# A fused cross-attention kernel on one core: the same operations by another table of turns

## The chip, the core and the metric

The kernel runs on one core of a Trainium2 chip. A core has five engines with a queue of instructions each: TensorE (PE in the profile; its weight loads are listed apart as PEld), VectorE (DVE), ScalarE (ACT), GpSimd (POOL) and SyncE (SP, which only issues transfers here). Each engine works through its queue in order and waits on semaphores where it needs another's result. Matrix products are written to PSUM, in banks of 128 x 512 float32. The metric is the time of one launch in microseconds of the device; less is better.

## The reference

Two batches of 2048 rows of 640 (`x`), and 128 rows of context of 384 per batch, the last four of which are "adapter" tokens. There are 8 heads of 80. All of it is float32. Cut to what matters:

```python
query = x @ Wq;  keyt = enc[:, :124] @ Wk;  valt = enc[:, :124] @ Wv
hs = mha(query, keyt, valt)                        # text: 2048 x 124 scores per head
ca = enc[:, 124:]
ca_q1 = einsum('btc,th->bch', ca, Wq_ca)[:, indices]   # 2048 rows, picked from 384
ca_hs1 = mha(ca_q1, x, x)                          # adapter: against the 2048 rows of x
ca_hs2 = mha(ca_hs1 @ Wq, ca @ Wk_ca, ca @ Wv_ca)  # 4 tokens
out = (hs + ca_hs2) @ Wout + b_out + x
```

Only 384 rows of the adapter's queries differ, so the kernel computes these and adds the right one to each row of the output at the end, by an indirect transfer of GpSimd.

## The kernel before, in words

**Work.** After a setup (weights turned and rearranged, text keys and values, 0 to about 60 us) the rows of `x` come in eight blocks of 512. Each block gives the adapter's two operands (`pyz`, `yz`, `zop`, `y_sb`) and the queries (`pq`, summed by reads into the tile `q`). The text attention works in 16 units of 256 rows, each with two halves of 128 ("softmax" tasks): scores `sc` on PE, row maxima `m` on DVE, exponentials with their sums on ACT (`p`), reciprocals `r` on DVE, then the shares (`p` times `r`; the function `share` may run on POOL, DVE or ACT), a transposition on DVE (`eb`), a store and a turned reload (`kept`, `pT`) through DRAM on SP. Then PE multiplies the probabilities by the values (`ph`), and ACT or DVE copies these into `hs`.

**Output.** For each unit the products of `hs` with `Wout` (`po`) and, for most blocks, those of the queries (`pq`) are made with seven half-size products instead of eight. That needs sums of quarters beforehand (`hs` sums s1 to s4, `wout_sums`, `x_sums`, each by POOL or DVE) and additions of results into the rows afterwards (DVE, `last_rows` and `x_more`). The rows begin as the residual, loaded by SP; when a tile of 128 rows has all its additions, POOL adds the adapter's rows by an indirect transfer (`add_second`, DMA_INDIRECT in the profile), and SP or ACT issues the store to the output.

**Adapter.** For each batch (`adapter`) PE makes scores twice. The first time, four 512-wide products (`s`) into one four-bank tile that exists once (`quad`), of which DVE takes the maxima (`mx`) and frees the tile; 24 of these groups for each batch. The second time ACT exponentiates the tile (`ea`), and PE contracts it with `y_sb` (`acc`); again 24 groups.

**Shapes of the PE array.** PE is used as tiles of 128x32, 32x128, 64x128, 64x32 or 128x128 rows and columns; `pq`, `po`, `ph` and `acc` are 128x32, the adapter's `s` is 32x128, the text scores `sc` 64x128, transpositions 128x128.

**What sets the order.** The tasks are Python generators that yield operations (`Do`) to a planner, `Desk`, which emits the instructions. Every operation belongs to a task with a path (`.56.3` is the third fork of the 56th task), and the table `TURNS` has for each path a list of turns, one for each operation of the task. A turn is one number that says two things: turn modulo 6 is the engine (PE, ACT, DVE, POOL, SP, or NONE for an operation without an instruction), and the order of turns is the order of emission, hence of each engine's queue. `run` takes the waiting operation with the lowest turn and gives it to `issue`, which emits it and keeps a planned time. That planned time decides one thing on the chip: `Room.take` gives an operation those buffers (PSUM banks, row slots, tiles) that the planner thinks are free earliest. All waiting on the chip is by semaphores that follow the data.

The paths that the prediction's steps touch:

- `.55.1`: the first scores and maxima of the adapter of the second batch (from about 280 us); turns 8022, 8160 and 8298 are the score groups at 305.82, 309.49 and 313.15 us.
- `.54`: the fifth column product of the last block's queries; `.54.7.3`: one of its chains; `.56.3`, `.60.3`, `.58.3`: the `ph` products of units 0, 4 and 2; `.68.2` and `.67.2`: text scores.
- `.60.3.4`: the sum s3 of `hs` of unit 4; `.60.3.12` and `.60.3.13`: the `po` products at 334.24 and 332.30 us.
- `.76.1` to `.76.4`: the four `wout_sums`.
- The last step of `stored` (paths such as `.62.3.10`): the stores of the output, "ACT" or "SP".

Every vector, scalar and GpSimd instruction shows line 427 in the profile (the helper `__getattr__`), products show 396 (`matmul`) or 405 (`by_columns`), transpositions 410, transfers 447 (`dma`), and GpSimd's indirect transfer 2351. So tiles are told apart by their names.

Of the kernel before, what the change touches and what calls it, by code (L numbers as in the profile page):

```python
# [8 lines left out]
F32 = mybir.dt.float32  # L9
# [5 lines left out]
P = 128  # L15
# [44 lines left out]
class Task:  # L60
    def __init__(self, gen, rank, key, more):
        self.gen, self.rank, self.key, self.more, self.last = gen, rank, key, more, Event()
        self.forks, self.ops, self.path = 0, 0, ""


class Desk:
# [242 lines left out]
    def begin(self, gen, rank):  # L309
        name = gen.__name__  # L310
        n = self.begun[name] = self.begun.get(name, -1) + 1
# [77 lines left out]
    def streamed(self, rhs):  # L389
        n = 1  # L390
# [69 lines left out]
def kernel(  # L460
# [15 lines left out]
    B, S, H = x.shape  # L476
# [2115 lines left out]
```

## Time and profile before

| | before |
|---|---|
| median of three runs | 573.39 us (572.63 to 573.96) |
| span of the profiled execution | 571.3 us |
| the profiled execution's own whole time | not given; the median is 2.1 us above the span |
| PE busy | 563.6 us (99%), 8069 instructions |
| DVE, ACT, POOL busy | 394.4, 286.7, 159.8 us |
| maxima of the adapter (`mx`) | 48 of 2271 ns on DVE |
| exponentials of the adapter (`ea`) | 48 of 1884 ns on ACT |
| DMA | 113.21 MB, 198 GB/s on average |

The profile gives one execution. Busy time is the union of an engine's instructions; ends of matrix products are modelled, so small stalls of PE do not always show as idle time. In a row of the timeline stand the start, the length, the engine, the line of the kernel, the operation, output and inputs, the shape, and the number of instructions put together; a bracket says how long the engine idled before it and who released it. In a table by stage each engine has its busy time within the stretch.

### The profile page before, as it was taken

To read this page: it belongs to the slowest core of one execution; us is meant where nothing else is said; L and a number is where in the kernel's file an instruction comes from. 1 tells how busy PE (TensorE), PEld (TensorE's weight loads), DVE (VectorE), ACT (ScalarE), POOL (GpSimd) and SP (SyncE) were. 2 spreads that over 40 slices of the span, in tenths; PEclk is the share of its full clock that TensorE was granted. 3 is DMA by queue.
4 is the path that set the end of the run, shared out by engine and by line. 5 is a ranking of instruction groups with operands and counts; after the bars stand their busy time and mean duration, and the time that the engine had idled before them with its cause. 6 is when DMAs were issued, how large, how long until landed. Compare 5 with 4: busy or idle time off the path is not lost.

```text
span 571.3 us, 18875 instructions
## 1 busy us (share of the span) xinstructions
PE 563.6 (99%) x8069; PEld 310.0 (54%) x8069; DVE 394.4 (69%) x659; ACT 286.7 (50%) x806; POOL 159.8 (28%) x213
## 2 busy tenths in 40 slices
PE   9999999999999999999999999999999999999997
PEld 8885335455555455466554554554555554445553
DVE  4366999999998577458999999998332213544443
ACT  2021355645566899899876654524554664100000
POOL 9102041114440731100004350531203053045152
PEclk9999999999999999999999999999999999999999
DMA  8998576965968977446746969977476587799888
GB/s 246 211 248 126 139 161 157 172 179 139 211 212 153 215 182 211 146 126 198 233 158 203 316 180 319 245 217 230 96 263 120 164 206 223 248 211 213 258 156 237
DMA packets 145691, 113.21 MB, mean 198 GB/s; under 512 B 82548, under 2 KB 116980, under 8 KB 145608
## 3 DMA queue, kind: packets, MB, share of 16 engines
q1 hardware_dynamic: 137000, 95.10, 60.0%
q0 software_dynamic: 5632, 10.69, 11.7%
q10 hardware_dynamic: 2976, 6.23, 3.2%
q8 instruction: 63, 1.03, 0.8%
q14 instruction: 20, 0.16, 0.1%
HBM read 71.60 MB, written 40.39 MB: 196 GB/s over the span
## 4 chain that ended last, share of the span: by engine, by line
PE 92%; DVE 3%; ACT 3%; DMA 1%; issue 1%; SPq 0%; ACTq 0%; DVEq 0%
PE po L405 27%; PE pq L405 24%; PE sc L396 7%; PE acc L396 7%; PE s L396 7%; PE ph L396 6%; PE pq L396 4%; PE pyz L396 2%; ACT ea L427 2%; DVE mx L427 2%; PE pv L396 1%; PE pk L396 1%; DMA xz<-in_x_dram 1%; ACT p L427 1%; PE pt_wq L410 1%
## 5 line engine op out<-in xcount | busy, mean ns | idle before, releaser
L427 ACT ACTIVATE p<-sc,m 128x124 f32<-128x124 f32 x256 | 90.1, 381 | 43.4 <-DVE m L427 38.4
L427 DVE TENSOR_REDUCE mx<-s 128x4 f32<-128x2048 f32 x48 | 109.0, 2271 | 1.9 <-PE s L396 1.9
L427 ACT ACTIVATE ea<-s 128x2048 f32<-128x2048 f32 x48 | 90.5, 1884 | 31.4 <-PE s L396 30.9
L405 PE MATMUL po<-wout_sums,hs 128*32 128x320 f32 x1024 | 78.5, 434 | 0.1
L405 PE MATMUL po<-wout_sb,hs 128*32 128x320 f32 x928 | 72.4, 433 | 0.0
L427 POOL TENSOR_TENSOR p<-p,r 128x992 f32<-128x992 f32 x17 | 31.4, 1847 | 130.9 <-DVE r L427 130.9
L405 PE MATMUL pq<-xt,wq_sb 128*32 128x256 f32 (+1 forms) x928 | 66.4, 418 | 0.0
L427 DVE TENSOR_TENSOR last_rows<-last_rows,po 128x320 f32<-128x320 f32 x60 | 28.1, 480 | 44.0 <-PE po L405 43.9
L427 ACT ACTIVATION_READ_ACCUMULATOR p<-sc,m 128x1 f32 x256 | 57.0, 223 | 0.0
L427 DVE TENSOR_TENSOR x_more<-x_more,po 128x320 f32<-128x320 f32 x68 | 32.4, 481 | 34.5 <-PE po L405 32.5
L405 PEld LDWEIGHTS po<-wout_sums,hs 128*32 128x32 f32 x1024 | 33.4, 110 | 32.7 <-issue 2.8
L427 DVE TENSOR_REDUCE m<-sc 128x4 f32<-128x496 f32 x64 | 40.8, 663 | 14.1 <-PE sc L396 14.0
L396 PE MATMUL acc<-ea,y_sb 128*32 128x384 f32 (+2 forms) x768 | 50.2, 382 | 0.2 <-ACT ea L427 0.2
L396 PE MATMUL ph<-pT,vpad 128*32 128x256 f32 x768 | 47.9, 381 | 0.0
L405 PEld LDWEIGHTS po<-wout_sb,hs 128*32 128x32 f32 x928 | 30.1, 110 | 28.2 <-issue 1.6
L2351 POOL DMA_INDIRECT x_more<-o,query x17 | 26.6, 1563 | 67.0 <-DVE x_more L427 31.1
L405 PEld LDWEIGHTS pq<-xt,wq_sb 128*32 128x32 f32 x928 | 27.7, 110 | 28.0 <-issue 13.4
L427 ACT COPY hs<-ph 128x512 f32<-128x512 f32 (+1 forms) x25 | 13.4, 551 | 57.7 <-PE ph L396 57.7
L427 DVE STREAM_TRANSPOSE eb<-p 128x1024 f32<-128x1024 f32 x32 | 39.4, 1233 | 1.2 <-POOL p L427 1.1
L396 PEld LDWEIGHTS sc<-kmain,q 64*128 64x128 f32 x512 | 31.8, 187 | 12.6 <-issue 5.8
L427 POOL TENSOR_TENSOR hs<-hs 128x256 f32<-128x256 f32 x31 | 28.9, 1019 | 33.9 <-ACT hs L427 25.6
L396 PE MATMUL sc<-kmain,q 64*128 64x124 f32 x512 | 38.0, 285 | 0.0
(219 smaller groups left out, 835.0 us busy)
## 6 DMA issues: line engine op xcount, KB each, us to landing
kept<-eb SPq DMA_DIRECT2D x32, 512.0 KB
pT<-kept SPq DMA_DIRECT2D x16, 1024.0 KB
landing<-away SPq DMA_DIRECT2D x15, 512.0 KB
xi<-in_x_dram SPq DMA_DIRECT2D x56, 128.0 KB
x_more<-in_x_dram SPq DMA_DIRECT2D x17, 320.0 KB
last_rows<-in_x_dram SPq DMA_DIRECT2D x15, 320.0 KB
y<-yt SPq DMA_DIRECT2D x16, 256.0 KB
y_sb<-y SPq DMA_DIRECT2D x32, 128.0 KB
```

Source lines behind the costliest of these rows:

```text
L396: self.pin(self.nc.tensor.matmul(out, lhsT, rhs, **kw))
L405: self.pin(self.nc.tensor.matmul(out[j : j + 32], lhsT[:, j : j + 32], rhs, **kw))
L410: self.pin(self.nc.tensor.transpose(out, in_, ident))
L427: self.pin(getattr(engine, what)(*args, **kw))
L2351: desk.pin(nc.gpsimd.indirect_dma_start(out=t, out_offset=None, in_=o2_of[b], in_offset=bass.IndirectOffsetOnAxis(ap=query[:, st : st + 1] ...
```

## The change

The table `TURNS` is replaced from turn 1141 on. The turns before are the same. 2281 turns stand in 617 paths, and 2021 of them have another number. 89 operations change their engine:

| from | to | number | what |
|---|---|---|---|
| ACT | DVE | 20 | copies of `ph` into `hs`, first reads of `pq`, two spreads of the text values, two copies of the adapter's result |
| DVE | POOL | 19 | sums of `hs`, of `x` and of `Wout`, two shares |
| POOL | DVE | 17 | the same kinds, two shares among them |
| DVE | ACT | 15 | copies and reads, one share |
| ACT | SP | 12 | stores of the output |
| ACT | POOL | 4 | shares |
| POOL | ACT | 1 | a share |
| SP | ACT | 1 | a half store of the output |

All others keep their engine, and many change their place in its queue. The planner is changed too: an operation without instruction holds back the later ones of its task and its forks (`placed`), planned times no longer rise with the turn (`run`), and some costs are other numbers (`streamed`; issue costs and latencies of transfers, of which a few are shown). The instructions emitted for an operation are the same.

```diff
-        self.forks, self.ops, self.path = 0, 0, ""
+        self.forks, self.ops, self.path, self.placed = 0, 0, "", None
...
+        task.placed = self.parent.placed
...
+        if task.placed is not None:
+            op.wait.append(task.placed)
+        if op.engines == ("NONE",):
+            task.placed = op.at
...
-            self.issue(max(self.ready(op), self.free[engine], self.now), engine, op)
+            self.issue(max(self.ready(op), self.free[engine]), engine, op)
...
-        return (max(n / 1.2, 106 if self.mode[1] > 32 else 27) + (9 if self.mode == (64, P) else 2.5)) / 1e3
+        return (max(n / 1.193, 106 if self.mode[1] > 32 else 27) + (9 if self.mode == (64, P) else 2.5)) / 1e3
...
-                    by_tokens[a], 0.67, 0.38, 1.7,
+                    by_tokens[a], 0.67, 0.56, 2.0,
...
-                dma(t, x[b, st * P : (st + 1) * P, :], 1.06, 0.37, 1.85)
+                dma(t, x[b, st * P : (st + 1) * P, :], 1.06, 0.38, 1.55)
...
-        desk.transfer("POOL", 2.0, 1.57, 2.2)
+        desk.transfer("POOL", 2.0, 1.57, 1.7)
```

The entries of the table that the text speaks of, each written on a line of its own (in `.55.1` the turns of the score groups and maxima around 300 to 318 us only):

```diff
-  ".54": [6215, 7055, 7373, 7812, 7968, 8040, 8057]
+  ".54": [5933, 7223, 7835, 7836, 7866, 7986, 8447]
-  ".54.7.3": [7740, 7902, 7932]
+  ".54.7.3": [7740, 7902, 8058]
-  ".55.1": [... 8022, 8048, 8160, 8222, 8298, 8324 ... 9234, 9284, 9318 ...]
+  ".55.1": [... 7980, 7994, 8166, 8174, 8262, 8270 ... 9264, 9272, 9354 ...]
-  ".56.3": [3275, 7079, 7132, 8100, 8124, 8184, 8339]
+  ".56.3": [7109, 7115, 7462, 8154, 8196, 8202, 8243]
-  ".60.3.4": [8870]        # DVE
+  ".60.3.4": [8745]        # POOL
-  ".60.3.12": [8898, 9086, 9108, 9152]
+  ".60.3.12": [8850, 8900, 8976, 8996]
-  ".60.3.13": [8844, 8906]
+  ".60.3.13": [8826, 8834]
-  ".67.2": [7650, 7854]
+  ".67.2": [7626, 7800]
-  ".67.3": [8543, 12509, 12520, 12966, 12978, 12990, 13001]
+  ".67.3": [9455, 12791, 12808, 12888, 12900, 12918, 12965]
-  ".76.1": [8150], ".76.2": [8115], ".76.3": [8205], ".76.4": [8277]
+  ".76.1": [8091], ".76.2": [8151], ".76.3": [8097], ".76.4": [8216]
-  ".62.3.10": [11069, 11085, 11161]   # a store, ACT
+  ".62.3.10": [11171, 11373, 11380]   # SP
```

More of the change, by code (lines that the diff above doesn't have):

```diff
@@ L1143, in keys @@
                     lambda i=i, e=e: dma(
-                        away[:, i, e].rearrange("q (g n) -> q g n", g=4), z[:, e].bitcast(F32), 0.45, 0.45
+                        away[:, i, e].rearrange("q (g n) -> q g n", g=4), z[:, e].bitcast(F32), 0.45, 0.6
                     ),
@@ L1272, in values_weights @@
             yield Do(
-                "SP", lambda g=g, cols=cols: dma(w2_sb[G * g : G * (g + 1)], rows_w2[:, :, cols], 0.45, 0.42),
+                "SP", lambda g=g, cols=cols: dma(w2_sb[G * g : G * (g + 1)], rows_w2[:, :, cols], 0.45, 0.62),
                 [("w2 out", g) for g in range(4)], marks=[("w2", g)],
@@ L1361, in of_pairs @@
                 d1 = VR + (R * i + VH) % P
-                dma(most[part, :2], v[:, 0::2, :, d0 : d0 + R], 1.7, 1.31)
+                dma(most[part, :2], v[:, 0::2, :, d0 : d0 + R], 1.7, 1.5, 1.6)
                 desk.pin(nc.sync.dma_start(most[part, 2:], v[:, 1::2, :, d1 : d1 + R]))
@@ L1369, in between_pairs @@
                     g = (0, 2, 1, 3)[i]
-                    dma(rest[part], w[:, :, D2 * g - VR : D2 * g + VR], 0.42, 0.45)
+                    dma(rest[part], w[:, :, D2 * g - VR : D2 * g + VR], 0.42, 0.95, 1.5)
                 else:
-                    dma(rest[part, :, :VR], w[:, :, H - VR :], 0.28, 0.46)
-                    dma(rest[part, :, VR:], w[:, :, :VR], 0.28, 0.46)
+                    dma(rest[part, :, :VR], w[:, :, H - VR :], 0.28, 0.8, 1.6)
+                    dma(rest[part, :, VR:], w[:, :, :VR], 0.28, 0.8, 1.6)
             op = yield Do("SP", between_pairs, [])
@@ L1709, in part_away @@
             def part_away(i, k=k, z=z):
-                dma(away[k, :, i].rearrange("q (g n) -> q g n", g=4), z[:, i].bitcast(F32), 0.48, 0.45, 1.6)
+                dma(away[k, :, i].rearrange("q (g n) -> q g n", g=4), z[:, i].bitcast(F32), 0.48, 0.59, 1.75)
             op = yield Do("ACT", lambda: desk.a_copy(z[:, 0], pq[:, cols]), [at], rank=0)
@@ L1736, in rest_back @@
         yield Do(
-            "SP", lambda: dma(t.rearrange("p g n -> p (g n)"), by_rows, 2.0, 0.56), [op.at], marks=[("landed", m)],
+            "SP", lambda: dma(t.rearrange("p g n -> p (g n)"), by_rows, 2.0, 0.6, 1.7), [op.at], marks=[("landed", m)],
             rank=0,
@@ L1848, in away @@
             def away(t=op.value, u=u):
-                dma(kept[:, :, u, :], t.rearrange("p (a n) -> p a n", a=4), 0.9, 0.53, 1.6)
+                dma(kept[:, :, u, :], t.rearrange("p (a n) -> p a n", a=4), 0.9, 0.58, 1.65)
             yield Do("SP", away, frees=[(yts, op.slots[0][0])], marks=[("y out", b, sb, u)], rank=0.5)
```

394 rows, old and new, of the table TURNS are left out of this document.

## The prediction

> **What bounds the kernel now.** I read the page's head, its tenths and its chain first.
>
> ```profile
> span 571.3 us, 18875 instructions
> PE 563.6 (99%) x8069; PEld 310.0 (54%) x8069; DVE 394.4 (69%) x659; ACT 286.7 (50%) x806; POOL 159.8 (28%) x213
> PE   9999999999999999999999999999999999999997
> DVE  4366999999998577458999999998332213544443
> PE 92%; DVE 3%; ACT 3%; DMA 1%; issue 1%; SPq 0%; ACTq 0%; DVEq 0%
> ```
>
> PE is the bound: 99% busy, 92% of the chain that ended last. The 3% each of DVE and ACT are places where PE stood still for them. An order can win only two things: those places, and PE's cost of changing from one array shape to another. The tenths show where the second engine is full: DVE holds 9s in slices 5 to 12 and 19 to 28. A table by stage makes that sharper (PE, PEld, DVE, ACT, POOL busy, each with its count).
>
> ```profile
> core 0: us, PE busy (x) PEld busy (x) DVE busy (x) ACT busy (x) POOL busy (x), PEclk, DMA share, GB/s
> 264.00:281.00 17.00, 16.43 (x261) 9.68 (x263) 14.52 (x22) 16.86 (x56) 1.28 (x1) 1.00 0.71 230
> 281.00:345.00 64.00, 62.75 (x932) 33.47 (x928) 62.86 (x76) 40.87 (x158) 20.53 (x18) 1.00 0.69 212
> 400.00:540.00 140.00, 139.84 (x2209) 70.61 (x2205) 51.73 (x116) 53.02 (x44) 38.40 (x32) 1.00 0.74 198
> ```
>
> PE idles 1.25 us in 281 to 345, where DVE has 62.86 of 64; it idles 0.57 in 264 to 281, where ACT has 16.86 of 17; in the 140 us after 400 it idles 0.16. The clock is full throughout. Ends of matmuls are modelled, so I measure a stall from start to start against the same group elsewhere, which finds more than the idle column does.
>
> The profiled span is 571.29 us, the median of the runs 573.39, so 2.1 lies around the span. I make the sum in the span and add it to the median.
>
> **The change, part by part.** Both tables are the same up to turn 1141. After it the kinds and numbers of operations are the same: 542 steps on PE, 374 to 355 on ACT, 566 to 569 on DVE, 107 to 112 on POOL, 306 to 317 on SP. The other constants only shape the planner's clock, and reach the chip through which buffer an operation is given. So I price the order on PE, then what each moved step makes PE wait for.
>
> *Changes of shape.* Counted from the two tables, PE leaves the 128x32 shape 104 times instead of 106.
>
> ```profile
> 401.09 1.05 PE L396 MATMUL ph<-pT,vpad 128*32 128x256 f32 x16
> 402.06 0.55 PE L396 MATMUL s<-cop,zop 32*128 32x128 f32 x8
> 413.83 1.05 PE L396 MATMUL acc<-ea,y_sb 128*32 128x256 f32 x16
> 414.70 0.72 PE L405 MATMUL po<-wout_sums,hs 128*32 128x320 f32 x8
> ```
>
> Sixteen 128x256 products take 0.97 before another shape and 0.87 before the same one: 0.10 for an exit, two fewer, **-0.20**.
>
> *The stall chain near 307 to 313.* Score groups (`s`) share one four-bank tile, freed by DVE's `mx`; so PE must put enough between two of them.
>
> ```profile
> 307.13 1.91 PE L396 MATMUL ph<-pT,vpad 128*32 128x256 f32 x32
> 309.49 0.51 PE L396 MATMUL s<-zop,cop 32*128 32x512 f32 x4 [0.45 <-DVE mx L427]
> 309.93 1.07 PE L396 MATMUL ph<-pT,vpad 128*32 128x256 f32 x16
> 310.93 1.16 PE L396 MATMUL sc<-kmain,q 64*128 64x124 f32 x16
> 313.15 0.50 PE L396 MATMUL s<-zop,cop 32*128 32x512 f32 x4 [0.66 <-DVE mx L427]
> 403.44 1.91 PE L396 MATMUL ph<-pT,vpad 128*32 128x256 f32 x32
> 405.27 0.45 PE L396 MATMUL s<-cop,zop 32*128 32x384 f32 x4
> 262.46 1.16 PE L396 MATMUL sc<-kmain,q 64*128 64x124 f32 x16
> 263.95 0.33 PE L396 MATMUL s<-cop,zop 32*128 32x128 f32 x4
> 303.51 2.00 DVE L427 SCALAR_TENSOR_TENSOR zop<-zop,low_z,zb 128x512 fp32r<-128x512 f32 x1
> 306.59 0.64 DVE L427 TENSOR_TENSOR q<-q,pq 128x512 f32<-128x512 f32 x1
> 307.16 2.27 DVE L427 TENSOR_REDUCE mx<-s 128x4 f32<-128x2048 f32 x1
> 310.86 2.23 DVE L427 TENSOR_REDUCE mx<-s 128x4 f32<-128x2048 f32 x1
> 303.41 1.55 POOL L427 TENSOR_TENSOR wout_sums<-wout_sb 128x640 f32<-128x640 f32 x1 [0.63 <-PE pq L405]
> L427 DVE SCALAR_TENSOR_TENSOR zop<-zop,low_z,zb x4: 725/744/1997, 295.1 to 338.4; 128x512 fp32r<-128x512 f32 x4
> ```
>
> `sc` to the next `s` is 1.49 undisturbed (262.46 to 263.95) and 2.22 here (310.93 to 313.15): 0.73 lost. Two `ph` to `s` is 1.83 (403.44) and 2.36 here (307.13): 0.53 lost. Both rows name `mx`.
>
> The second: the score at 309.49 is done at 310.00, `mx` starts 0.86 late (310.86), runs 2.23, and 0.06 later PE goes on; from score to score 3.66. The work between was 0.44 + 1.00 + 1.49 = 2.93. The new order puts a second `ph` there (turns 8196 and 8202 between 8166 and 8262): 0.44 + 1.83 + 1.49 = 3.76, more than 3.66 even with DVE as late as now. **-0.73**, from 0 if DVE comes 0.8 later still.
>
> The first: the work between the scores keeps its length, so only an earlier `mx` helps. DVE runs without a gap from 303.51; the addition into `q` (0.64) goes behind that `mx`, and `zop`, 2.00 against a median of 0.744 while POOL reads beside it, is to come when POOL's `wout_sums` (moved behind others, turn 8151) has not begun: 0.64 + 1.25 earlier could be had, more than 0.53. But `eb` still waits for POOL's share, and DVE waits in order behind it. Between 0 and 0.53, I take half, **-0.25**.
>
> *332 to 334.*
>
> ```profile
> 332.30 1.26 PE L405 MATMUL po<-wout_sb,hs 128*32 128x320 f32 x16
> 333.18 0.91 DVE L427 TENSOR_TENSOR hs<-hs 128x256 f32<-128x256 f32 x1
> 334.24 1.28 PE L405 MATMUL po<-wout_sums,hs 128*32 128x320 f32 x16
> 460.97 1.28 PE L405 MATMUL po<-wout_sb,hs 128*32 128x320 f32 x16
> 462.61 0.29 PE L396 MATMUL acc<-ea,y_sb 128*32 128x128 f32 x4
> ```
>
> The 24 products take 1.64 at 460.97 and 1.94 here. The next product reads the sum that DVE ended at 334.09. That sum goes to POOL, some seven us ahead of its reader: **-0.30**. POOL idles 43 of these 64 us, which hides it; without that cover it would be late by its POOL length.
>
> *173.7.*
>
> ```profile
> 173.72 1.05 PE L405 MATMUL pq<-xt,wq_sb 128*32 128x256 f32 x16
> 174.71 0.42 PE L405 MATMUL pq<-x_sums,wq_sb 128*32 128x256 f32 x4
> ```
>
> 0.99 against 0.87 for the same shape (413.83): 0.12, with another group put between: **-0.12**.
>
> *The 264 to 281 stage.* Order and engines of PE and ACT are the same in both tables here: 0; its idle 0.57 bounds a gain.
>
> *New tight place.* Near 345 two scores (turns 9264 and 9354) have between them only their own 0.44, an output product of 16 (1.1, from the rows above) and a score product (1.49): 3.0. They need 0.51 + 2.25 + 0.06 = 2.82 and DVE's lateness, for which I take 0.4: **+0.2**. With DVE as late as at 310.86 it would be +0.7, with DVE on time 0.
>
> *Shares, copies and sums on other engines (77 steps).* Their own length lies beside PE. Four softmax shares leave ACT for POOL and one goes the other way; I find no reader on PE that follows at once. They cost nothing as long as POOL's queue is not held by a gather.
>
> *Twelve stores from ACT to SP, one back.* Each waits on its queue for POOL's gather, and SP holds the loads behind it.
>
> ```profile
> 430.86 1.55 POOL L2351 DMA_INDIRECT x_more<-o,query  x1 [0.16 <-issue]
> 436.31 0.37 ACTq L447 DMA_DIRECT2D out_dram<-x_more  x1
> 454.99 0.38 SPq L447 DMA_DIRECT2D pT<-kept  x1
> 463.47 0.40 PE L396 MATMUL ph<-pT,vpad 128*32 128x256 f32 x4
> ```
>
> A store follows its gather by 5.45. The one at 436.31 now stands on SP, with a residual load and this `pT` load behind it; the load had 8.48 to its first product. Working down the new order (the gather after the sum of the copies of `ph` for unit 3, then 5.45, then the two loads), I get the issue about nine us ahead of that product: as much as now. The same at 498 to 522, where three stores and two residual loads come ahead of the last but one `pT`. I take 0; the cover is what those 8.48 leave above the transfer, and SP being held for one gather more (5.45) would use it up.
>
> *Tail.*
>
> ```profile
> 566.66 1.03 DVE L427 TENSOR_TENSOR x_more<-x_more,po 128x320 f32<-128x320 f32 x2 [0.61 <-PE po L405]
> ```
>
> Both tables end with a product, an addition and half a tile stored; 0.
>
> Sum: -0.20 - 0.73 - 0.25 - 0.30 - 0.12 + 0.20 = **-1.4**, span 569.9, time **572.0**.
>
> **The rivals.** *A, the gains are handed on (DVE is the pace).* DVE holds 62.86 of 64 us in the stage where 1.28 of the 1.6 us lie. The change takes 20 steps to DVE from ACT and 17 from POOL there and elsewhere, and gives 34 away; if DVE's sum of work in the stage stays, each `mx` is late again at the next tight score. Left would be shape changes and the step at 173.7: -0.3, 573.1. For it: the stage's DVE has only 1.14 us free. Against: in the places above, the new spacing covers DVE's present lateness.
>
> *B, more than forecast.* The 0.57 idle of the ACT-paced stage goes too, and the first stall wholly (0.28 more), and the new tight place costs nothing (0.2): -2.4, 571.0. For it: earlier stages leave the queues ahead. Against: same order there.
>
> *C, slower: DVE and POOL meet more often.* The `zop` row is the price: 2.00 against 0.744, 1.25 a meeting, while POOL reads for 1.55. The change puts sums with two inputs on either side (19 to POOL, 17 to DVE). Three more meetings in 281 to 345 are 3.75 us on a DVE with 1.14 free: 2.6 on PE, and the gains of that stage gone: 573.4 - 0.3 + 2.6 = 575.7; it decides from the second meeting on (574.5). Against: `wout_sums`, the longest of these, moves away from `zop`. The Trainium skill, SBUF — State Buffer, "Who interferes with whom", says that a VectorE instruction with two SBUF inputs contends with a GpSimd one that reads SBUF and that the loser waits for the whole instruction; by that, an estimate, a meeting costs up to the 1.55 of the POOL row, and three would give 576.6; the trace's loss of 1.25 agrees with it in kind.
>
> *D, slower: SP held.* One `pT` load behind a late gather, 5.45 less the cover; the cover is unknown, and half of the price gives 573.4 - 1.4 + 2.7 = 574.7. PE in 400 to 540 has no slack (139.84 of 140) to take it.
>
> *E, it doesn't do what it says:* the dearer issues and the port are only in the planner; a table searched with them may be no better on the chip. Then shape changes are left and new stalls balance old: 573.2, together with A.
>
> **How the numbers follow.** Forecast 0.40; A and E 0.30; B 0.11; C 0.12; D 0.07. A measurement of this kernel can tell about 0.2%, 1.15 us, from no change: below 572.24 is faster, above 574.54 slower. The forecast, 0.2 below that line, is faster in about 0.37 of its 0.40, rounded for its spread of 0.8; with B and a few of A's cases 0.50. C and D, less some that end inside, 0.18. The rest, 0.32, is no change. The range goes from 570.2 (B with the half spread of the runs before, 572.63 to 573.96) to 574.7 (D); C's upper part and what lies under B are left out. The forecast's own range is 571.2 to 572.8.
>
> **What would show it.** In the profile after: the idle of PE in the stage around 281 to 345 falls from 1.25 to about 0.3; `sc` to `s` is 1.49 where the row names no `mx`; the `zop` operations stay near 0.744; the waits of weight loads for ACT's `ea` stay. Wrong would be: stalls before `s` rows with `mx` elsewhere in that stage (A), DVE sums of twice their median (C), or a `ph` or `po` that waits for SP (D).

## Result, and the profile after

The changed kernel takes 576.14 us (median, 576.03 to 577.57), the kernel before 573.21 beside it (572.63 to 573.96): 1.006 of its time, 95% interval 1.0045 to 1.0075. It is slower by 2.9 us, where 1.4 us less was forecast, and the range ended at 574.7.

The head of the page after, its tenths of PE and DVE and its chain:

```profile
span 574.5 us, 18855 instructions
PE 565.0 (98%) x8069; PEld 308.8 (54%) x8069; DVE 395.3 (69%) x666; ACT 280.3 (49%) x780; POOL 168.5 (29%) x218
PE   9999999999999999899999999999999999999997
DVE  4366999999999465477899999898532232544443
PE 72%; DVE 12%; ACT 6%; SPq 4%; DMA 3%; issue 2%; DVEq 0%; ACTq 0%
```

PE's row has one 8, in slice 17, about 230 to 244 us. In the chain PE fell from 92% to 72%, and DVE and ACT together rose from 6% to 18%. The table by stage says where (PE, PEld, DVE, ACT, POOL busy); first the kernel before, in the two stages that the prediction did not show:

```profile
60.00:180.00 120.00, 120.00 (x1686) 59.29 (x1678) 117.06 (x153) 64.21 (x245) 32.12 (x24) 1.00 0.72 171
180.00:264.00 84.00, 83.82 (x1368) 46.65 (x1367) 54.84 (x94) 75.47 (x184) 19.79 (x24) 1.00 0.68 179
```

Then the kernel after:

```profile
60.00:180.00 120.00, 118.65 (x1661) 59.17 (x1657) 117.12 (x156) 61.66 (x237) 31.68 (x23) 1.00 0.73 172
180.00:264.00 84.00, 82.28 (x1326) 45.87 (x1326) 49.96 (x91) 68.41 (x164) 27.21 (x28) 1.00 0.61 168
...
281.00:345.00 64.00, 63.12 (x939) 34.00 (x935) 61.30 (x73) 37.88 (x149) 22.21 (x21) 1.00 0.75 233
400.00:540.00 140.00, 139.49 (x2202) 69.55 (x2198) 56.60 (x122) 54.50 (x42) 38.80 (x32) 1.00 0.71 196
```

Between 60 and 264 us PE idled 0.18 us; now it idles 3.07 (1.35 + 1.72). The stage of 281 to 345, where most of the gain was forecast, did get better, from 1.25 to 0.88. So the time went where the prediction had priced nearly nothing. The two largest of the new stalls, from the timeline after (rows of other steps are left out; a loss is measured from the start of a group of products to the start of the next one, against the same group without a stall). Near 93 us:

```profile
91.45 2.30 DVE L432 TENSOR_REDUCE mx<-s 128x4 f32<-128x2048 f32 x1
92.43 0.38 ACT L432 CAST x_sums<-pq 128x256 fp32r<-128x256 f32 x1
92.92 1.91 PE L410 MATMUL pq<-xt,wq_sums 128*32 128x256 f32 x32
93.64 0.43 DVE L432 TENSOR_TENSOR x_sums<-pq,x_sums 128x256 fp32r<-128x256 f32 x1
94.11 0.37 ACT L432 CAST wq_sums<-pq 128x256 fp32r<-128x256 f32 x1 [1.30 <-DVE x_sums L432]
95.06 0.59 ACT L432 COPY q<-pq 128x512 f32<-128x512 f32 x1
95.80 1.50 PE L410 MATMUL pq<-x_sums,wq_sums 128*32 128x256 f32 x24 [0.97 <-ACT q L432]
```

Read it from the last row back. PE wants the tile that ScalarE's copy `q` empties. The copy stands on ScalarE behind the second cast of the query remainder (`halves_away`), with two exponentials between them; the cast waited 1.30 for VectorE's first subtraction, and the subtraction stood behind the maximum `mx`. The cast does not use what the subtraction writes: the one reads columns 256 to 511 of the PSUM tile `pq`, the other columns 0 to 255. Thirty-two such products take 1.73 elsewhere; here 2.88 pass to the next start, so 1.15 is lost. (The 1.73 is seen below, from 93.16 to 94.89 in the run with the casts first.)

Near 237 us, the second:

```profile
236.98 1.93 PE L410 MATMUL pq<-x_sums,wq_sums 128*32 128x256 f32 x32
237.09 0.23 DVE L432 RECIPROCAL r<-pt_acc 128x12 f32<-128x12 f32 x1 [3.41 <-PE pt_acc L415]
237.84 0.37 DVE L432 TENSOR_TENSOR x_sums<-pq,x_sums 128x256 fp32r<-128x256 f32 x1
238.24 0.37 ACT L432 CAST wq_sums<-pq 128x256 fp32r<-128x256 f32 x1 [1.67 <-DVE x_sums L432]
238.51 1.88 ACT L432 ACTIVATE ea<-s 128x2048 f32<-128x2048 f32 x1
240.45 0.51 PE L401 MATMUL s<-cop,zop 32*128 32x256 f32 x8 [1.54 <-ACT ea L432]
```

The same wait, 1.67, behind a reciprocal that waited 3.41 for PE; and this time the exponential `ea` stands behind the cast. It frees the score tile for the next `s`. From 236.98 to 240.45 are 3.47, against 1.86 without the wait (237.74 to 239.60 in the run with one block, below): 1.61 lost.

The kernel before has the wait too. Its row at the same step:

```profile
94.53 0.40 DVE L427 TENSOR_TENSOR x_sums<-pq,x_sums 128x256 fp32r<-128x256 f32 x1
94.97 0.37 ACT L427 CAST wq_sums<-pq 128x256 fp32r<-128x256 f32 x1 [0.68 <-DVE x_sums L427]
96.88 0.58 ACT L427 COPY q<-pq 128x512 f32<-128x512 f32 x1 [1.54 <-PE pq L405]
```

The cast starts 0.04 after the subtraction ends, and 0.03 or 0.04 after it in five more of the seven blocks of queries that do this step; in the seventh, near 236 us, `ea` and another cast stood ahead of it. Here it cost nothing because no one wanted what stood behind it: the next copy waited 1.54 for PE anyway. In the built programs of both kernels the second cast waits for VectorE's first subtraction of the same tile in all seven blocks.

The planner knows no such edge. In its account only ScalarE's queue puts the second cast behind the first; the wait is added when the program is built. So it is not true of this wait that all waiting on the chip follows the data. The Trainium skill, PSUM — Partial Sum Buffer, "PSUM bank collisions raise a hardware error", says that ScalarE and VectorE may not touch the same PSUM bank in the same 32 partitions at one time, reads by both included, and that a semaphore has to keep them apart whether or not they touch the same bytes. The tile is 512 columns of 4 bytes, one bank of 2 KiB by the section "Terms" of that page. The traces agree as far as they go: in none of the seven blocks of either kernel do the two reads overlap. What would happen if they did, no run here shows, and that this rule is why the build adds the wait is likely but not shown: further down, a copy of `po` waits in the same way, although the two copies read different banks.

Smaller losses behind the same wait: 0.51 at 153.7, 0.26 at 163.9, and 0.41 at 196.8 beyond what was there before. With the two above this is 3.94. The first 1143 operations of the table before are the same work in both orders; the group of scores behind them starts at 262.46 us before and at 266.46 in the new order: 4.0 later.

### The profile page after: what moved, and what is told of

Same layout as the page of the kernel before. It is cut to its first block, busy times and chain, and to the rows that moved or that the text cites. A ratio compares the mean times of both kernels' runs of the same rounds, so it can differ in the third digit from the quotient of the medians.

```text
span 574.5 us, 18855 instructions
## 1 busy us (share of the span) xinstructions
PE 565.0 (98%) x8069; PEld 308.8 (54%) x8069; DVE 395.3 (69%) x666; ACT 280.3 (49%) x780; POOL 168.5 (29%) x218
## 3 DMA queue, kind: packets, MB, share of 16 engines
q8 instruction: 63, 1.03, 0.7%
## 4 chain that ended last, share of the span: by engine, by line
PE 72%; DVE 12%; ACT 6%; SPq 4%; DMA 3%; issue 2%; DVEq 0%; ACTq 0%
PE po L410 28%; PE pq L410 11%; PE ph L401 7%; PE acc L401 7%; PE s L401 5%; DVE mx L432 5%; PE sc L401 4%; SPq L452 4%; PE pq L401 4%; ACT ea L432 3%; PE pyz L401 2%; ACT p L432 2%; DVE eb L432 1%; DVE xt L432 1%; DVE m L432 1%
## 5 line engine op out<-in xcount | busy, mean ns | idle before, releaser
L432 POOL TENSOR_TENSOR p<-p,r 128x992 f32<-128x992 f32 x20 | 37.8, 1893 | 129.9 <-DVE r L432 116.4
L432 DVE TENSOR_TENSOR x_more<-x_more,po 128x320 f32<-128x320 f32 x72 | 34.0, 481 | 54.0 <-PE po L410 53.5
L410 PE MATMUL po<-wout_sb,hs 128*32 128x320 f32 x896 | 69.3, 434 | 0.1
L410 PEld LDWEIGHTS po<-wout_sums,hs 128*32 128x32 f32 x1024 | 31.3, 110 | 35.0 <-issue 3.2
L432 POOL TENSOR_TENSOR hs<-hs 128x256 f32<-128x256 f32 x32 | 24.6, 800 | 84.7 <-DVE hs L432 69.1
L432 DVE TENSOR_TENSOR last_rows<-last_rows,po 128x320 f32<-128x320 f32 x56 | 26.8, 483 | 29.2 <-PE po L410 28.0
L401 PE MATMUL ph<-pT,vpad 128*32 128x256 f32 x768 | 46.3, 380 | 0.0
L410 PEld LDWEIGHTS po<-wout_sb,hs 128*32 128x32 f32 x896 | 28.0, 110 | 29.3 <-issue 2.6
L2356 POOL DMA_INDIRECT x_more<-o,query x18 | 28.8, 1602 | 40.3 <-DVE x_more L432 28.0
```

The costliest lines, as they stand in the source:

```text
L401: self.pin(self.nc.tensor.matmul(out, lhsT, rhs, **kw))
L410: self.pin(self.nc.tensor.matmul(out[j : j + 32], lhsT[:, j : j + 32], rhs, **kw))
L432: self.pin(getattr(engine, what)(*args, **kw))
L2356: desk.pin(nc.gpsimd.indirect_dma_start(out=t, out_offset=None, in_=o2_of[b], in_offset=bass.IndirectOffsetOnAxis(ap=query[:, st : st + 1] ...
```

## Experiments

Each ratio is to the kernel before, timed on the same chip beside the run (medians 572.94 to 573.37). Where times of different chips and the ratios disagree, the ratio is the better measure.

**Which part of the table: two crossings.** The tables are cut at operation 1143 of before (the edits of these two runs are given in words). First the order before up to there, then the new one, with the new code:

```diff
-  all operations: turns of the new table
+  operations up to 1143: turns of the table before; the rest: new table
```

> A table put together from both: the 1143 operations of before up to turn 6856 (TensorE at 262.5 us), then the rest by the new table. By the two traces the first part of the new table takes 4.0 us more (262.46 against 266.46) and the rest the same (304.7 in both). Theory 1 and theory 2: 573.2 (572.6 to 573.8), the loss lies wholly in the first part. If the first part's order hands something on that the rest needs, 574.5 or more.

Measured: 572.55 us, ratio 0.9999 (0.999 to 1.0008). Then the new order up to the cut, and the order before after it, with the code before:

```diff
-  all operations: turns of the table before
+  operations up to the cut: new table; the rest: turns of the table before
```

> The other half: the new table up to its turn 6857, then the table of before. Theories 1 and 2: 573.2 + 4.0 = 577.2 (576.6 to 577.9). If part of the loss were in the rest, 576 or less.

Measured: 576.43 us, ratio 1.0068 (1.0054 to 1.0082). The whole loss is in the first part. The second part alone makes no difference that can be told. (Both times lie up to 0.2 us under the ranges expected; by the ratios they are inside.)

**The wait taken away, not the order.** The changed kernel, with both casts given to ScalarE before VectorE's first subtraction in the seven blocks; the turns of these steps follow, the queues of PE, VectorE, POOL and SP stay as they are, and on ScalarE the only change of order is one cast that passes a copy of `q`.

```diff
-            op = yield Do("ACT", lambda: desk.a_copy(z[:, 0], pq[:, cols]), [at], rank=0)
-            main_at = op.at
-            op = yield Do("DVE", lambda: desk.b_tensor_tensor(..., ALU.subtract), rank=0, ...)
+            op = yield Do("ACT", lambda z=z, cols=cols: desk.a_copy(z[:, 0], pq[:, cols]), [at], rank=0)
+            casts.append((k, z, cols, part_away, op.at))
...
+        for of_one in casts if n else ():
+            yield from subtract(*of_one)
-  ".24.5": [2171, 2173, 2180, 2189, 2191, 2198]
+  ".24.5": [2171, 2173, 2177, 2179, 2180, 2198]
```

> The changed kernel, with one thing undone: in each of the seven blocks after the first, ScalarE's second cast of the query remainder is emitted ahead of VectorE's first subtraction instead of behind it, so the program no longer makes that cast wait for VectorE. All other queues keep their order. Theory 1 (a wait that the planner doesn't count: ScalarE's cast holds its queue until VectorE has subtracted, and the read or the exponential behind it comes late for TensorE): the starts show stalls of 1.15 us near 93, 1.61 near 237, 0.26 near 164 and 0.41 more than before near 197; most of this 3.4 goes, 576.1 becomes 573.0 (572.6 to 573.7). Theory 2 (VectorE is simply too full between 60 and 264 us, and whoever reads its results is late whatever stands in ScalarE's queue): the stalls stay or move, 575.5 or more.

Measured: 572.13 us, ratio 0.9987 (0.9978 to 0.9996), span 570.4: a little more than the whole loss, and 0.5 under the range expected. The same edit on the kernel before, as a control:

> The kernel before with the same edit: the second cast ahead of the first subtraction. The control: there the subtraction stands right behind its cast, ScalarE waits 0.4 to 0.9 us and no TensorE stall is found behind it in the trace. Theory 1: the same as before within 0.4 us (572.8 to 573.5). If casts first were good in itself (less waiting on ScalarE anywhere), it would gain 1 us or more.

Measured: 572.53 us, ratio 1.0002 (0.9993 to 1.0011), as expected by the ratio and 0.3 under the range in us. The edit is worth nothing to the old order and 4.0 us to the new one (576.14 - 572.13; by the ratios 1.006 and 0.9987 it is 4.2). The timeline of the first of them at the step near 93 us:

```profile
92.67 0.38 ACT L428 CAST x_sums<-pq 128x256 fp32r<-128x256 f32 x1
92.92 0.41 ACT L428 CAST wq_sums<-pq 128x256 fp32r<-128x256 f32 x1
93.16 1.91 PE L406 MATMUL pq<-xt,wq_sums 128*32 128x256 f32 x32
93.88 0.42 DVE L428 TENSOR_TENSOR x_sums<-pq,x_sums 128x256 fp32r<-128x256 f32 x1
94.89 1.91 PE L406 MATMUL pq<-x_sums,wq_sums 128*32 128x256 f32 x32
```

The subtraction is as late as before (93.88), the cast no longer waits for it, and PE goes from 93.16 to 94.89 without a stall. The stall near 237 is gone as well.

**The cause put into the kernel before.** If the late subtraction with its wait is the price, one such move in the kernel before must cost the same. Its first subtraction at 94.53 goes behind the maximum that follows:

```diff
-  ".24.5": [2213, 2239, 2258, 2267, 2269, 2366]
+  ".24.5": [2213, 2239, 2310, 2267, 2269, 2366]
```

> The kernel before, with the suspected wait made longer in one block: VectorE's first subtraction (at 94.53 us) stands behind the reciprocal, the transposition and the maximum that followed it, as in the new table. All of ScalarE's and TensorE's queues are as before. Theory 1: ScalarE's second cast waits for it until about 98.3 instead of 94.9, the read behind it ends near 99.3 instead of 97.5, and TensorE stands still for some 1.9 us before the product at 97.5: 574.9 (574.2 to 575.4). Theory 2 (what costs is a late VectorE, not the wait): the subtraction itself is read by nobody soon, 573.0 (within 0.4).

Measured: 576.09 us, ratio 1.0041 (1.0027 to 1.0055), so 2.4 us from one turn of one operation (3.0 by the medians, above the range expected). In the built program only VectorE's queue differs: the subtraction stands behind a reciprocal, a transposition and the maximum. (2310 is a turn of PE by its remainder, but only the planner's account books the step there; the next run does so too.) Its timeline:

```profile
98.39 1.05 PE L401 MATMUL pq<-xt,wq_sb 128*32 128x256 f32 x16
99.67 0.41 DVE L423 TENSOR_TENSOR x_sums<-pq,x_sums 128x256 fp32r<-128x256 f32 x1
100.11 0.37 ACT L423 CAST wq_sums<-pq 128x256 fp32r<-128x256 f32 x1 [4.07 <-DVE x_sums L423]
101.03 1.93 PE L401 MATMUL pq<-x_sums,wq_sums 128*32 128x256 f32 x32 [1.59 <-ACT q L423]
```

The chain of the changed kernel stands in the old one: subtraction, cast 4.07 late, `q`, PE. Start to start it is 1.78 lost. This profiled execution, the slowest of the five, also lost about 1.5 near 60 and 72 us, where VectorE and then ScalarE waited 1.84 and 1.70 for transfers. Whether the 0.6 between 1.78 and 2.4 comes from there stays open.

The same late subtraction, with the casts first in all seven blocks, by the code shown above (the turns of the one block):

```diff
-  ".24.5": [2213, 2239, 2258, 2267, 2269, 2366]
+  ".24.5": [2213, 2239, 2255, 2257, 2310, 2366]
```

> The same late subtraction, with the second cast ahead of it in the program, so that ScalarE doesn't wait for it. Theory 1: the stall is gone, 573.0 (572.4 to 573.4). If the late subtraction costs by itself (the bank or the transfer behind it), about the time of the run without the casts moved.

Measured: 573.26 us, ratio 0.9998 (0.9989 to 1.0007). That VectorE comes late costs nothing here; what costs is that ScalarE waits for it.

**One of the seven blocks.** The changed kernel with the casts first only in the block near 237 us. In the built program every engine's queue is then the same as in the changed kernel; only this one wait is gone:

```diff
+            if n != 6:
+                yield from subtract(*casts[k])
+        for of_one in casts if n == 6 else ():
+            yield from subtract(*of_one)
```

> The changed kernel with the second cast ahead in one block only, the one near 237 us, where the start-to-start stall is 1.61. Theory 1: 576.1 - 1.6 = 574.5 (574.1 to 575.0), the other stalls of the first part stay. Theory 2: 576.1.

Measured: 575.24 us, ratio 1.0035 (1.0024 to 1.0047): 1.4 of the 3.4 us (0.0025 of the ratio) come from that block; by the medians only 0.8, and the time is above the range expected. Its trace has the undisturbed step:

```profile
237.74 1.93 PE L406 MATMUL pq<-x_sums,wq_sums 128*32 128x256 f32 x32
239.60 0.51 PE L397 MATMUL s<-cop,zop 32*128 32x256 f32 x8
```

The next scores come 1.86 later, and the stall at 92.85 is there with 1.15. The execution has a stall of its own, 0.90 at 207 us, after VectorE had waited 1.75 for a transfer, which may hide part of the 1.61.

**What is left: a meeting at 290 us and a tile at 498 us.** With the casts first, two stalls of 0.6 remained that the kernel before does not have. The first is seen in the timeline of the changed kernel:

```profile
289.86 1.84 POOL L432 TENSOR_TENSOR p<-p,r 128x992 f32<-128x992 f32 x1 [5.76 <-DVE r L432]
290.20 1.61 DVE L432 TENSOR_TENSOR p<-p,r 128x96 f32<-128x96 f32 x1
291.96 0.64 PE L401 MATMUL pt_p<-ident,p 128*32 128x128 f32 x16 [0.43 <-DVE p L432]
```

A scaling of 128x96 takes 1.61 on VectorE and ends about where POOL's scaling ends, beside which it ran. The second, in the same timeline:

```profile
496.59 0.69 ACT L432 COPY o<-po 128x640 f32<-128x640 f32 x1 [1.47 <-PE po L401]
497.32 0.82 DVE L432 COPY o<-po 128x640 f32<-128x640 f32 x1 [1.05 <-ACT o L432]
498.20 0.81 PE L401 MATMUL po<-w_sb,p2T 32*128 32x320 f32 x4 [0.51 <-DVE o L432]
```

ScalarE and VectorE each copy a part of one tile `po`, and VectorE waits 1.05 for the other engine before it begins. It has the form of the casts' wait, but not its likely reason: `po` is a tile of four banks here (`tile([P, 4, 512])`), and each copy reads two banks of its own (`q4[:, 2 * c : 2 * c + 2, :HALF]`). Why the build orders these two is open. The kernel with three repairs has the casts first, VectorE's reciprocal (the one that releases POOL) behind that scaling, and a product of the output put ahead of the one that needs the tile:

```diff
-  ".65.2.2": [..., 7453, 7490, 7569, ...]
+  ".65.2.2": [..., 7453, 7514, 7569, ...]
-  ".68.3.11": [12246, 12284, 12366, ...]
+  ".68.3.11": [12246, 12284, 12312, ...]
```

> The changed kernel with casts first in seven blocks, and two more stalls taken away: the reciprocal that releases GpSimd's share behind the small two-input product near 290 us (1.61 us there against 0.26 in the trace of before, while GpSimd reads; TensorE loses 0.6), and one output product more between the two rounds of the adapter's second output near 496 us, where VectorE's copy waits for ScalarE's (TensorE loses 0.58). From 572.1 of casts first: 572.1 - 0.6 - 0.58 = 571.0 (570.6 to 571.6). If VectorE is the pace between 281 and 345 us the first of the two moves on to the next score group: 571.5.

Measured: 570.64 us, ratio 0.9963 (0.9949 to 0.9976): faster than both kernels. Without the last of the three:

> The changed kernel with two of the three repairs of the run with all three: the second cast on ScalarE of the query remainder ahead of the first subtraction on VectorE in all 7 blocks, and the reciprocal near 237 us put behind the second product, so that the scaling at 290 us no longer meets that of POOL. Theory: the meeting at 290 us cost 0.6 us of its own (the stall there ahead of pt_p was 0.59 in the kernel with the casts alone, which took 0.9987 of the time before), so 571.5; the remaining 0.6 to 0.9 of the kernel with all three repairs (570.64) is then the PSUM tile of the second projection. Rival: the stall at 290 us is given back at the next reads of the score tile, and the time stays at the 572.1 of the casts alone.

Measured: 571.37 us, ratio 0.9966 (0.9952 to 0.998). (The reciprocal that its expectation puts near 237 us is the one shown at the meeting.) Its timeline there:

```profile
286.77 0.26 DVE L428 TENSOR_TENSOR p<-p,r 128x96 f32<-128x96 f32 x1
287.29 1.84 POOL L428 TENSOR_TENSOR p<-p,r 128x992 f32<-128x992 f32 x1 [6.55 <-DVE r L428]
288.00 0.62 PE L397 MATMUL pt_p<-ident,p 128*32 128x128 f32 x16
```

VectorE first, POOL after it: 0.26 for 1.61, and PE does not wait. The time is 0.76 below the casts alone (572.13), or 1.2 by the ratios, whose intervals just touch; the stall was 0.6. The last repair is 0.73 by the medians, but by the ratios (0.9963 and 0.9966) it can't be told from nothing; that its stall of 0.58 is gone shows only in the trace.

**The planner's side of the change.** The new table with the code and prices before:

```diff
-        if task.placed is not None:
-            op.wait.append(task.placed)
...
-                    by_tokens[a], 0.67, 0.56, 2.0,
+                    by_tokens[a], 0.67, 0.38, 1.7,
...
```

> The new table of turns with the code and the planner prices of before: only what these prices choose (buffer slots, PSUM banks) differs from the changed kernel. Theory: the table alone makes the change slower, so 576.1 with the same stalls near 93, 154, 164 and 237 us. Rival: the dearer issues of SyncE in the account of the planner choose other slots and cost part of the 2.9 us; then 573.2 to 575.

Measured: 581.8 us, ratio 1.0126 (1.0105 to 1.0148). Both theories missed it, and the direction too: with the old prices the new table is 5.7 us slower still (3.8 by the ratios). Its timeline:

```profile
316.74 2.90 PE L401 MATMUL po<-wout_sb,hs 128*32 128x320 f32 x40
321.94 2.36 PE L401 MATMUL po<-wout_sums,hs 128*32 128x320 f32 x16 [2.30 <-DVE x_more L423]
```

and that of the changed kernel at the same step:

```profile
316.54 2.90 PE L410 MATMUL po<-wout_sb,hs 128*32 128x320 f32 x40
319.50 1.28 PE L410 MATMUL po<-wout_sums,hs 128*32 128x320 f32 x16
```

The queues of all engines hold the same steps in the same order; what differs is which tile a step is given (PSUM tiles, and the slots of `pT`), and so what it waits for. Here PE waits 2.30 for VectorE's read by `x_more`, which does not hold it in the changed kernel. Start to start, 4.1 are lost from there to 324 (2.48, 1.03, 0.55) where the changed kernel loses 0.5, and 0.8 and 0.4 more at 393 and 447: 4.8 of the 5.7. The stalls at 92.89 (1.15) and 237.20 (1.61) are the same as in the changed kernel. The counterpart, the old table with the new code:

> The table of turns of before with the code and the planner prices of the changed kernel: the other half of the change alone, the counterpart of the run with the new table and the old code (581.8). Theory: code and table go together; the planner prices only choose which PSUM banks and buffers an operation is given, and the old table was made with the old prices, so it loses some of what it had: 573.5 to 576, with stalls at products that wait for a read of the tile they are given. Rival: the new prices choose better slots for any table, or the same ones; then 572.5 to 573.2.

Measured: 572.56 us, ratio 0.9992 (0.998 to 1.0004). There the rival holds: the old table gains or loses nothing by the new prices. So the new prices belong to the new table, in its second half; by themselves they do nothing that can be told.

## Why the prediction was wrong

*The step that failed* is the second half of "So I price the order on PE, then what each moved step makes PE wait for". It was done for steps that change their engine and for places behind 264 us. A step that keeps its engine and only moves within its queue was put at nothing, without a reason, from turn 1141 to 264 us, where the working looked only at 173.7. VectorE's first subtraction is such a step. And where the working asked for readers ("I find no reader on PE that follows at once"), it asked who reads the moved step's own result. That the subtraction's own result comes late cost nothing (573.26 with the casts first). The cost is that `q` or `ea` comes late: they stand behind ScalarE's second cast, which waits for the subtraction without using its data.

PE's idle of 0.18 us between 60 and 264 says that nothing can be won there; it also says that there was little room for a new wait of PE. The row that would have told was in the trace before: a cast that begins 0.03 or 0.04 after a subtraction on another engine ends, six times in seven, is likely waiting for it. What stands behind the cast can be read from the new table.

In place of nothing, the wait costs 3.94 by the stalls and 4.0 by the run with the casts first, nearly the whole error of 4.1 (576.14 against 572.0). The sum of all that was found closes: 3.94 of this wait, 1.74 of the second half (below), less 1.5 of the terms that were named, make 4.2, and PE's last product ends 4.04 later (567.14 before, 571.18 after).

*The terms that were named* came near, as this timeline of the changed kernel shows:

```profile
308.70 0.51 PE L401 MATMUL s<-zop,cop 32*128 32x512 f32 x4
310.88 1.05 PE L401 MATMUL ph<-pT,vpad 128*32 128x256 f32 x16
312.08 0.51 PE L401 MATMUL s<-zop,cop 32*128 32x512 f32 x4 [0.15 <-DVE mx L432]
314.41 1.16 PE L401 MATMUL sc<-kmain,q 64*128 64x124 f32 x16
316.11 0.50 PE L401 MATMUL s<-zop,cop 32*128 32x512 f32 x4
```

The second stall of the chain: `sc` to `s` is 1.70 where 1.49 is undisturbed, so 0.21 is left of 0.73; forecast -0.73, got -0.52. The order did cover VectorE's lateness, and the rest has no `mx` in its row. The first: `ph` to `s` is 1.20 against 0.97, 0.23 left of 0.53; forecast -0.25, got -0.30. 332 to 334: the wait is gone; the same 24 products take 1.63 at 334.88 (-0.31 for -0.30). 173.7: gone (-0.13 for -0.12). The tight place near 345 shows no stall (0 for +0.2). Two exits from the 128x32 shape fewer, 104 for 106 in the built programs: by the starts of this trace 0.10 to 0.13 an exit, -0.20 to -0.26 for -0.20; no run isolates it. Together about -1.5, against -1.4. That the sums agree so well is in part luck: the second stall gave 0.21 less than forecast, and the tight place cost 0.2 less. (The counts given as those after turn 1141, 542 on PE and so on, are those of the whole table; after it PE has 477. Their differences are the same.)

That sum did not arrive even where the first part was left out: the kernel with the old order up to the cut was at 0.9999 of before. Its second half gives the gains back at the scaling beside POOL (0.60), the tile `po` (0.58) and two groups of output products between 316.5 and 320.9 us (0.25 and 0.31), none of them named. The first is shown by the run that takes it away (its trace and, just, its time), the second by its trace alone; the other two were not tried.

*The other zeros.* SP: in no place after does a product wait for a load that SP held, so rival D did not happen and its cover was enough. The stage that is paced by ScalarE around 270 us: its three stalls have 0.20, 0.15 and 0.22 before and after the change, no gain, as taken. The tail: 4.2 us from PE's end to the span's end before, 3.3 after; the experiments that keep the old second half show 3.4 to 3.8, so most of this is likely the one execution that was profiled.

*The rivals.* B did not happen: the idle of the stage that ScalarE paces stayed. A needs `mx` late at the next tight scores; one row near 312 us has it, with 0.23 left, and A's 573.1 was passed for another reason. C had the right side and the wrong place: its mechanism is real, one meeting of 1.61 against 0.26 costs 0.6 us of PE, but in the scaling at 290 and not in `zop` (0.71 now at 309.11), and it is the smaller part. The Trainium skill, SBUF — State Buffer, "Who interferes with whom", has the one that issues first hold the shared ports for its whole instruction, and the other wait; the 1.35 lost beside a POOL instruction of 1.84 that had begun 0.34 earlier, and so had 1.50 to go, agrees. E was right that a table searched with a better account of transfers and the port need not be better on the chip; what it named, new stalls against old, is what happened, at a price that its 573.2 did not hold.

## What to carry to other kernels

Two engines that read one PSUM tile were a chain in this program, though its schedule did not count it: when the first reader is put later, everything behind the second in its queue goes with it. So look in a profile for an instruction that starts within 0.04 us of another engine's end each time; it is likely waiting for it, and that costs nothing only while nothing behind it in its queue is wanted soon. Price a moved step by who waits for it in each queue, above all in the stages without idle time, and let one engine take all its reads of the tile first (here both casts before the subtraction: 4.0 us).

## What the runs showed of the hardware that was not expected

A tile of PSUM that two engines read in disjoint columns was read by one after the other, by a wait that the build puts into the program: gap 0.04 us at 94.97 before, waits of 1.30, 1.67 and 4.07 where the first reader was late, and 1.05 between the copies of `po`, which lie in different banks. No run has the two read at once. A choice of tiles alone, with the same order on every engine, moved this kernel by 5.7 us (576.14 to 581.8; 3.8 by the ratios). And a small scaling on VectorE, 0.26 us by itself, took 1.61 beside a scaling on POOL.
